# Placing the recurrence's steps by a running count of matrix products beside the gather, and a gate spread over two ticks

## The chip, the cores and the metric

The kernel runs on one core of one Trainium2 chip. The metric is the device time of one execution in microseconds, from the first to the last instruction with what lies around it; lower is better. The core has a matrix engine (PE, with its weight loads listed apart as PEld), a vector engine (DVE), a scalar engine (ACT), a general engine (POOL) and a queue that issues transfers (SP). Each takes its own instructions strictly in the order in which the program wrote them, and waits on semaphores for the others.

## What is computed

Four layers on an input of 8 images x 128 channels x 64 x 64, each on a group-normalised input and added to it:

```python
x = x + layer0(gn(x))   # a state-space scan along 4096 positions, and a 3x3 convolution
x = x + layer1(gn(x))   # four recurrences, below
x = x + layer2(gn(x))   # t3 (two column convolutions) times t4 (a small product)
x = x + layer3(gn(x))   # deformable 3x3 convolution, then a batch norm

# layer 1: down, up, right, left; 63 steps each, every one needs the one before
new = cur + relu(conv1d(prev, w))          # 9 taps along the row

# layer 3: per output pixel 9 taps, each from 4 corners at computed positions
samp = corner(y0, x0, ...) + corner(y0, x0+1, ...) + corner(y0+1, x0, ...) + corner(y0+1, x0+1, ...)
out = einsum(samp * mask, dcn_w)
```

## The kernel before, in words

All is float32. Layer 1 works on four images at once that lie in one tile X, so it runs twice: images 0 to 3, then images 4 to 7. The second run is a generator (`propagate`, called `one`): each `next(one)` writes out one **step**, that is 9 products of 128x128 by up to 256 columns on PE into `ps_l1` (each float32 product is two instructions, 18 in the trace, L913) and one DVE instruction (L920) that adds the result into X. The next step's products read what that DVE instruction wrote. A direction has 63 steps and one turn that only loads weights: 64 turns, 256 in all.

Beside this second run go layer 2 and layer 3 of the first images. The order of the work is written out by hand in **ticks**: one loop over n (before the change its body is at L133 to L155), 96 ticks per image, whatever stands in tick n being written out in this order:

1. `three.tick`, layer 3, from tick 96 on. `fetch` issues 3 gathers (POOL, L1264; an indirect transfer of 128 rows of 2 KB each) into a buffer `got`, of which there are GOT = 6. Then come the parts held back from earlier ticks: `convolve` of four ticks ago (18 PE instructions, L1317, in every sixth tick, n % 6 == 3), `turn` of the fetch two ticks ago (3 PE transposes, L1304, which free the `got` buffer), `keep` (ACT, L1311) and `sum` of the fetch one tick ago (2 DVE additions, L1297). Then `weigh` of this tick's fetch (1 DVE product L1282, 3 ACT products L1286).
2. What `Layer2.plan` puts into the tick for the image that is to be gathered next. Its image has 8 row groups g, four ticks apart (t = 4g): `x2_load` at t-4 (SP), `x2_norm` at t-2 (ACT), `t1_product` at t (PE, L1044), `t4_product` at t+1 (PE, L1058), `t3_start` at t+2 (ACT, L1068), `t3_gate` at t+3 (four DVE instructions, L1073, L1075, L1076, L1077, and the store of the result), `x3_stats` at t+5 (DVE). From tick 36 follow the normalisation, the `tokens` (PE transposes, ACT, table stores), the `offsets` (PE, L1138) and the sampling positions (DVE).
3. A step of layer 1, if the tick has one. In ticks below 96 every third tick has one. From tick 96 to tick `last` = 4 * 96 + 30 = 414 every tick whose number is not a multiple of three has one (`if n % 3: next(one, None)`, L141 to L143 before). At tick 414 any remaining step is written out, and the rest of the loop (ticks to 863) has no steps: X then holds the finished layer 1 and gives way, and later gathers go into pieces of X.

So the part around the change is ticks 96 to 413: image 0 is gathered in ticks 96 to 191 while layer 2 works on image 1, and so on; from tick 384 layer 2 has no work until tick 433. For image 4 (`b == NB2`) two plan times go into one tick. The PSUM buffers that matter: tag `l2a` (two buffers: `ps_t1`, `ps_t3`, `ps_tok`, ...), tag `l2b` (one buffer: `ps_t4`, `ps_off`), `ps_l1` (one), `ps_s` (three). Tile `x2` and tile `t3` have two buffers each.

Of the kernel before, what the change touches and what calls it, by code (L numbers as in the profile page):

```python
# [10 lines left out]
F32 = mybir.dt.float32  # L11
I32 = mybir.dt.int32
AF = mybir.ActivationFunctionType
ALU = mybir.AluOpType
# [3 lines left out]
P = 128  # L18
B, C, H, W = 8, 128, 64, 64
# [5 lines left out]
TR = T // W  # L25
NCH = HW // T
# [13 lines left out]
@with_exitstack  # L40
def conv_preact_kernel(ctx: ExitStack, tc: tile.TileContext, a: dict, out: bass.AP):
    nc = tc.nc
    x_in = a["x"].rearrange("b c h w -> b c (h w)")
    y_out = out.rearrange("b c h w -> b c (h w)")

    const = ctx.enter_context(tc.tile_pool(name="const", bufs=1))
    dram = ctx.enter_context(tc.tile_pool(name="dram", bufs=1, space=DRAM))


    ident = const.tile([P, P], F32, name="ident")  # L50
    make_identity(nc, ident)

    gmat = const.tile([P, P], F32, name="gmat")
    nc.gpsimd.memset(gmat, 0.25)
    gview = gmat.rearrange("p (g q) -> p g q", q=4)
    nc.gpsimd.affine_select(
        out=gview, in_=gview, pattern=[[-4, 32], [0, 4]], compare_op=ALU.is_ge,
        fill=0.0, base=0, channel_multiplier=1,
    )
    nc.gpsimd.affine_select(  # L60
        out=gview, in_=gview, pattern=[[4, 32], [0, 4]], compare_op=ALU.is_ge,
        fill=0.0, base=3, channel_multiplier=-1,
    )
    eps = const.tile([P, 1], F32, name="eps")
    nc.gpsimd.memset(eps, 1e-5)

    x1d = [dram.tile([C, HW], F32, name=f"x1d{b}") for b in range(B)]
    x2d = [dram.tile([C, HW], F32, name=f"x2d{b}") for b in range(B)]
    od = [dram.tile([C, HW], F32, name=f"od{b}") for b in range(B)]
    x3d = [dram.tile([C, HW], F32, name=f"x3d{b}") for b in range(B)]  # L70
    cd = [dram.tile([P, T], F32, name=f"cd{c}") for c in range(B * HW // (4 * T))]
    wide = {
        name: [dram.tile([P, T], F32, name=f"{name}_{i}") for i in range(B * HW // T)] for name in ("dtd", "ud")
    }
    tables = [dram.tile([SIDE * DEEP, 2 * C], F32, name=f"table{b}") for b in range(B)]


    norm1 = const.tile([P, B, 2], F32, name="norm1")
    norm2 = {}
    with tc.tile_pool(name="x", bufs=1) as xp, tc.tile_pool(name="l1w", bufs=1) as wd, tc.tile_pool(  # L80
        name="l1ps", bufs=1, space=PSUM
    ) as pl:
        X = xp.tile([P, HW, NB2], F32, name="X")
        zero = layer0(tc, a, ident, gmat, x_in, x1d, cd, wide, norm1, X, pl)
        one = propagate(tc, a, wd, pl, X)
        edges = borders(tc, X, tables)
        for n in zero:
            with tc.manual_schedule():
                if n >= 0:
                    next(edges, None)  # L90
                if n >= READY:
                    next(one, None)
        with tc.manual_schedule():
            run(edges)
            run(one)

        st = const.tile([P, B * NCH, 6], F32, name="bn_st")
        with tc.tile_pool(name="l2w", bufs=1) as wp, tc.tile_pool(name="l2", bufs=2) as w2, tc.tile_pool(
            name="l3", bufs=2
        ) as w3, tc.tile_pool(name="l2ps", bufs=2, space=PSUM) as p2, tc.tile_pool(  # L100
            name="l3ps", bufs=3, space=PSUM
        ) as p3, tc.manual_schedule():
            st2 = [const.tile([P, NCH, 6], F32, name=f"st2_{b}") for b in range(B)]
            one = propagate(tc, a, wd, pl, X)
            next(one)
            for part in exchange(tc, w3, x1d, x2d, norm1, X, st2):
                if part >= 1:
                    next(one)
                    next(one)
            two = Layer2(tc, a, ident, gmat, eps, x2d, x3d, tables, norm2, wp, w2, p2)  # L110
            three = Layer3(tc, a, ident, tables, od, st, wp, w3, p3)

            def norm_of(b):
                n = group_norm(tc, w2, p2, gmat, eps, st2[b], "l2a")
                keep = const.tile([P, 2], F32, name=f"norm2_{b}")
                for i in range(2):
                    nc.vector.tensor_copy(keep[:, i : i + 1], n[i])
                norm2[b] = keep[:, 0:1], keep[:, 1:2]

            for b in range(NB2):  # L120
                norm_of(b)
            late = residual(tc, w3, x1d, x2d, X, st2, norm_of)

            plans = {}
            for b in range(B):
                for when, what in sorted(two.plan(b).items()):
                    n = b * two.TICKS + when
                    if b == NB2:
                        n = (b + 1) * two.TICKS - (two.TICKS - 5 - when) // 2
                    plans.setdefault(n, []).extend(what)  # L130
            last = NB2 * two.TICKS + 30
            for n in range(min(plans), (B + 1) * two.TICKS):
                b, i = n // two.TICKS - 1, n % two.TICKS  # L133
                if b >= 0:
                    three.tick(b, i, two.done[b], 2 if n < last else 0)
                for f in plans.pop(n, ()):
                    f()
                if n < two.TICKS:
                    if n % 3 == 0:
                        next(one, None)  # L140
                elif n < last:  # L141
                    if n % 3:
                        next(one, None)  # L143
                else:
                    if n == last:
                        run(one)
                        three.bank = pl
                    if n < last + 12 or n % 3 == 0:
                        if next(late, True) and not three.more:
                            size = 3 * 4 * C  # L150
                            flat = X.rearrange("p h b -> p (h b)")
                            for i in range(HW * NB2 // size):
                                piece = flat[:, i * size : (i + 1) * size]
                                three.more.append(piece.rearrange("p (k q c) -> p k q c", k=3, c=C))
                            three.turns = 0  # L155
            run(late)
            while three.late:
                three.tick()
    finish(tc, a, eps, od, x3d, y_out, st, const)
# [663 lines left out]
def run(thread):  # L823
    for _ in thread:
        pass
# [117 lines left out]
class Layer2:  # L943

    TICKS = 96

    def __init__(self, tc, a, ident, gmat, eps, x2d, x3d, tables, norm2, wp, w2, pp):
        self.tc, self.ident, self.gmat, self.eps = tc, ident, gmat, eps  # L950
# [48 lines left out]
    def plan(self, b):  # L999

        nc, w2, pp = self.nc, self.w2, self.pp
        events = {}

        def at(when, f, *args):
            events.setdefault(when, []).append(lambda: f(*args))

        rows = lambda ap: ap.rearrange("p (r w) -> p r w", w=W)
        x2_rows, x3_rows = rows(self.x2d[b]), rows(self.x3d[b])
        S = {}
# [56 lines left out]
        def t3_start(g):  # L1066
            acc = S["acc", g] = pp.tile([P, TR, W], F32, tag="l2a", name="ps_t3")
            nc.scalar.activation(acc, S["t1", g][:, 0:TR, :], AF.Identity, scale=self.w3[:, 0:1])  # L1068

        def t3_gate(g):  # L1070

            acc, t1, t4 = S["acc", g], S["t1", g], S["t4", g]
            nc.vector.scalar_tensor_tensor(acc, t1[:, 1 : 1 + TR, :], self.w3[:, 1:2], acc, ALU.mult, ALU.add)  # L1073
            t3 = w2.tile([P, TR, W], F32, name="t3")
            nc.vector.scalar_tensor_tensor(t3, t1[:, 2 : 2 + TR, :], self.w3[:, 2:3], acc, ALU.mult, ALU.add)  # L1075
            nc.vector.tensor_mul(t4, t3, t4)  # L1076
            nc.vector.tensor_add(t3, S["x2", g][:, 1 : 1 + TR, :], t4)  # L1077
            S["x3", g] = t3.rearrange("p r w -> p (r w)")
            nc.sync.dma_start(self.x3d[b][:, g * T : (g + 1) * T], S["x3", g])
# [124 lines left out]
        for g in range(NCH):  # L1204
            t = 4 * g
            at(t - 4, x2_load, g)
            at(t - 2, x2_norm, g)
            at(t, t1_product, g)
            at(t + 1, t4_product, g)
            at(t + 2, t3_start, g)  # L1210
            at(t + 3, t3_gate, g)
            at(t + 5, x3_stats, g)
        at(36, x3_load, 0)
        at(39, x3_norm_stats)
        for u in range(2):
            t = 44 + 16 * u
# [17 lines left out]
class Layer3:  # L1234
# [59 lines left out]
    def sum(self, got, sums):  # L1294
        for n in range(sums):
            q = 2 - n
            self.nc.vector.tensor_add(got[:, :, 0:q, :], got[:, :, 0:q, :], got[:, :, q : 2 * q, :])  # L1297
# [134 lines left out]
```

## Time and profile before

| | |
|---|---|
| median of 3 runs | 6828.69 us (6819.01 to 6831.93) |
| the profiled execution's own time | 6825.9 us |
| its span, first to last instruction | 6824.2 us |
| mean granted PE clock over the span | 0.877 |
| busy of the span: PE, DVE, ACT, POOL | 81%, 62%, 44%, 64% |
| L913, the steps' products (both runs of layer 1) | 9072 instructions, 2039.9 us |
| L1264, gathers into `got` (into X) | 1614 (690) instructions, 1098 (948) ns each |
| L1282, L1297, DVE per gathered buffer | 1351 ns; 761 ns twice (ticks below 414) |
| L1317, convolutions | 2304 instructions, 590.9 us |

How to read it: the span is that of one execution. "Busy" is the time in which an engine had an instruction in work; idle time stands in front of the instruction that ended it, with what released it. A tick can be found in the trace by counting: there are 768 products L1282, the i-th of them (from 0) is that of tick 96 + i; and the j-th group of three transposes L1304 is written out in tick 98 + j. A tick's length on PE is taken from one such group to the next. In the table by stretches the columns are: from and to, length, then busy time and number of instructions of PE, PEld, DVE, ACT and POOL, then the granted PE clock, the DMA engines' busy share and GB/s.

### The profile page before, as it was taken

To read this page: it belongs to the slowest core of one execution; us is meant where nothing else is said; L and a number is where in the kernel's file an instruction comes from. 1 tells how busy PE (TensorE), PEld (TensorE's weight loads), DVE (VectorE), ACT (ScalarE), POOL (GpSimd) and SP (SyncE) were. 2 spreads that over 40 slices of the span, in tenths; PEclk is the share of its full clock that TensorE was granted. 3 is DMA by queue.
4 is the path that set the end of the run, shared out by engine and by line. 5 is a ranking of instruction groups with operands and counts; after the bars stand their busy time and mean duration, and the time that the engine had idled before them with its cause. 6 is when DMAs were issued, how large, how long until landed. Compare 5 with 4: busy or idle time off the path is not lost. (4 is left out here: it accounts for less than half of the span.)

```text
span 6824.2 us, 76741 instructions
## 1 busy us (share of the span) xinstructions
PE 5519.9 (81%) x25628; PEld 3703.4 (54%) x25628; DVE 4206.7 (62%) x4615; ACT 3000.8 (44%) x5976; POOL 4342.3 (64%) x3758
## 2 busy tenths in 40 slices
PE   4778887799999999899989999977777777876670
PEld 1222222267676767667777777765645555555550
DVE  4889898877777773427677677766542343433235
ACT  4667777655454541313333333333433343433332
POOL 3778787766666662116776776787666666666655
PEclk7777677799999999899999999998888888987775
DMA  4556565544444441525666666667776666676658
GB/s 123 167 173 190 152 182 160 154 133 130 130 130 131 128 132 41 173 80 181 192 191 187 196 191 192 190 178 247 253 223 206 196 212 208 212 213 190 187 164 291
DMA packets 496236, 1195.66 MB, mean 175 GB/s; under 512 B 76248, under 2 KB 117152, under 8 KB 493792
## 3 DMA queue, kind: packets, MB, share of 16 engines
q0 software_dynamic: 184320, 604.13, 30.0%
q1 hardware_dynamic: 300000, 561.43, 26.9%
q10 hardware_dynamic: 11520, 25.18, 1.0%
q8 instruction: 204, 3.34, 0.2%
q14 instruction: 192, 1.57, 0.1%
HBM read 1031.24 MB, written 159.22 MB: 174 GB/s over the span
## 5 line engine op out<-in xcount | busy, mean ns | idle before, releaser
L1264 POOL DMA_INDIRECT got<-table,idx x1614 | 1772.6, 1098 | 1030.1 <-issue 469.4
L913 PE MATMUL ps_l<-X,w_dir 128*128 128x240 f32 (+4 forms) x9072 | 2039.9, 380 | 116.9 <-DVE X L920 75.7
L913 PEld LDWEIGHTS ps_l<-X,w_dir 128*128 128x128 f32 x9072 | 1715.3, 193 | 500.9 <-DVE X L920 186.7
L775 POOL TENSOR_TENSOR hb<-hb,C 128x1024 f32<-128x1024 f32 x512 | 1208.7, 2361 | 41.5 <-POOL carry L774 1.0
L769 DVE TENSOR_TENSOR_SCAN hb<-da,carry,ub_ps 128x512 f32<-128x512 f32 x896 | 1097.8, 1266 | 70.6 <-ACT da L752 13.9
L752 ACT ACTIVATE da<-dt_s,a_neg 128x512 f32<-128x512 f32 x1024 | 678.5, 715 | 569.4 <-DVE hb L769 523.8
L1264 POOL DMA_INDIRECT X<-table,idx x690 | 653.8, 948 | 355.3 <-issue 143.5
L920 DVE SCALAR_TENSOR_TENSOR X<-ps_l,X 128x256 f32<-128x256 f32 x504 | 213.2, 423 | 905.8 <-PE ps_l L913 736.1
L1311 ACT COPY samp<-ps_s 128x384 f32<-128x384 f32 x768 | 365.2, 476 | 860.1 <-remote 455.8
L1304 PE MATMUL ps_s<-ident,got 128*128 128x128 f32 x3594 | 540.9, 295 | 232.1 <-issue 122.7
L1286 ACT ACTIVATE got<-got,wgt 128x128 f32<-128x128 f32 x1614 | 556.7, 400 | 274.7 <-DMA got<-table,idx 220.9
L760 DVE TENSOR_TENSOR ub_ps<-u_s,B_ps 128x1024 f32<-128x1024 f32 x512 | 625.6, 1222 | 82.4 <-PE B_ps L541 52.6
L1317 PE MATMUL ps_o<-samp,dcn_w 128*128 128x256 f32 x2304 | 590.9, 407 | 101.9 <-issue 93.6
L1304 PEld LDWEIGHTS ps_s<-ident,got 128*128 128x128 f32 x3594 | 462.6, 153 | 325.9 <-issue 179.5
L1304 PE MATMUL ps_s<-ident,X 128*128 128x128 f32 x2760 | 424.1, 308 | 187.9 <-issue 166.5
L1317 PEld LDWEIGHTS ps_o<-samp,dcn_w 128*128 128x128 f32 x2304 | 459.7, 204 | 210.5 <-issue 138.5
L774 POOL COPY carry<-hb 128x2 f32<-128x2 f32 x512 | 95.7, 187 | 658.2 <-DVE hb L769 596.4
L1304 PEld LDWEIGHTS ps_s<-ident,X 128*128 128x128 f32 x2760 | 370.9, 161 | 246.8 <-issue 212.3
L1282 DVE TENSOR_TENSOR got<-got,wgt 128x1152 f32<-128x1152 f32 x336 | 453.7, 1351 | 78.0 <-DMA got<-table,idx 70.1
L1297 DVE TENSOR_TENSOR got<-got 128x768 f32<-128x768 f32 x636 | 484.1, 761 | 19.6
L784 PE MATMUL ps_y<-hb,m_y 128*32 128x512 f32 x2048 | 346.2, 742 | 54.4 <-DVE xc L558 41.2
L1282 DVE TENSOR_TENSOR got<-got,wps 128x1152 f32<-128x1152 f32 x202 | 264.4, 1343 | 203.3 <-ACT wps L1278 144.7
(222 smaller groups left out, 6029.8 us busy)
## 6 DMA issues: line engine op xcount, KB each, us to landing
dt_s<-dtd SPq DMA_DIRECT2D x512, 256.0 KB
u_s<-ud SPq DMA_DIRECT2D x512, 256.0 KB
table<-tok SPq DMA_DIRECT2D x128, 256.0 KB
got<-table,idx POOLq DMA_INDIRECT x1614
x<-x2d SPq DMA_DIRECT2D x48, 384.0 KB
x3h<-x3d SPq DMA_DIRECT2D x16, 1056.0 KB
dtd<-dt SPq DMA_DIRECT2D x64, 256.0 KB
ud<-u SPq DMA_DIRECT2D x64, 256.0 KB
```

The source lines that it names most:

```text
L752: nc.scalar.activation(da[:, k], steps[i]["dt"], AF.Exp, scale=a_neg[:, q, k : k + 1])
L760: nc.vector.tensor_mul(ub, st["u"].unsqueeze(1).to_broadcast([P, 2, T]), s["B", h])
L769: nc.vector.tensor_tensor_scan(hb[:, k, :], st["da"][:, k, :], ub[:, k, :], start, ALU.mult, ALU.add)
L775: nc.gpsimd.tensor_mul(hb, hb, S[c]["C", h])
L913: nc.tensor.matmul(ps[:, c0:c1, :], lhsT=w[:, k, :], rhs=v[:, prev, c0 + k - PAD : c1 + k - PAD, :], start=(k == PAD), stop=(k == K - 1),)
L1264: nc.gpsimd.indirect_dma_start(out=got[:, k, :, :].rearrange("p q c -> p (q c)"), out_offset=None, in_=self.tables[b], in_offset=bass.Indi ...
L1282: nc.vector.tensor_mul(got[:, :, 0:3, :], got[:, :, 0:3, :], w.unsqueeze(3).to_broadcast([P, G3, 3, C]))
L1286: nc.scalar.activation(got[:, k, 3, :], got[:, k, 3, :], AF.Identity, scale=wgt[:, t, k0 + k, 3:4])
L1297: self.nc.vector.tensor_add(got[:, :, 0:q, :], got[:, :, 0:q, :], got[:, :, q : 2 * q, :])
L1304: nc.tensor.matmul(ps[:, k, :], lhsT=got[:, k, q, :], rhs=self.ident, is_transpose=True, start=(q == 0), stop=(q == parts - 1),)
L1311: self.nc.scalar.copy(samp[:, k0 : k0 + self.G3, col : col + P], ps)
L1317: nc.tensor.matmul(ps, lhsT=self.dcn_w[:, k, :], rhs=samp[:, k, :], start=(k == 0), stop=(k == KK - 1))
```

## The change

Steps are no longer put into two of three ticks from tick 96 on. A table `load` says for each of the 318 ticks how many units of 128 columns of products it holds without a step: 2 for the transposes, 18 for a convolution, and for layer 2's parts what `PRODUCTS` says. A step is counted as 18. `pace` is the sum of all loads and of all steps still to come, divided by 318. Going through the ticks a running total of loads and placed steps is kept, and steps are written out in a tick as long as the total is half a step behind the pace: none, one or two.

Second, `t3_gate` is cut in two: its first two DVE instructions become `t3_sum` (still at t+3), and the last two and the store stay `t3_gate`, now at t+4; `x3_stats` goes to t+6 and the first `x3_load` to tick 37. No instruction is added or taken away.

```diff
             last = NB2 * two.TICKS + 30
+            STEP = 18
+            first = two.TICKS
+            load = {
+                n: 2 + 18 * (n % 6 == 3) + sum(f.products for f in plans.get(n, ())) for n in range(first, last)
+            }
+            steps, taken, total = 4 * H, 2 * NCH - 1, 0
...
                 if n < two.TICKS:
                     if n % 3 == 0:
-                        next(one, None)
+                        next(one)
+                        taken += 1
                 elif n < last:
-                    if n % 3:
-                        next(one, None)
+                    if n == first:
+                        pace = (sum(load.values()) + STEP * (steps - taken)) / (last - first)
+                    total += load[n]
+                    while total + STEP / 2 <= pace * (n + 1 - first) and taken < steps:
+                        next(one)
+                        taken, total = taken + 1, total + STEP
...
+    PRODUCTS = {"t1_product": 20, "t4_product": 12, "offsets": 14, "tokens": 2, "offsets_out": 2}
...
         def at(when, f, *args):
-            events.setdefault(when, []).append(lambda: f(*args))
+            what = lambda: f(*args)
+            what.products = self.PRODUCTS.get(f.__name__, 0)
+            events.setdefault(when, []).append(what)
...
+        def t3_sum(g):
+            acc, t1 = S["acc", g], S["t1", g]
+            nc.vector.scalar_tensor_tensor(acc, t1[:, 1 : 1 + TR, :], self.w3[:, 1:2], acc, ALU.mult, ALU.add)
+            t3 = S["t3", g] = w2.tile([P, TR, W], F32, name="t3")
+            nc.vector.scalar_tensor_tensor(t3, t1[:, 2 : 2 + TR, :], self.w3[:, 2:3], acc, ALU.mult, ALU.add)
+
         def t3_gate(g):
 
-            acc, t1, t4 = S["acc", g], S["t1", g], S["t4", g]
-            nc.vector.scalar_tensor_tensor(acc, t1[:, 1 : 1 + TR, :], self.w3[:, 1:2], acc, ALU.mult, ALU.add)
-            t3 = w2.tile([P, TR, W], F32, name="t3")
-            nc.vector.scalar_tensor_tensor(t3, t1[:, 2 : 2 + TR, :], self.w3[:, 2:3], acc, ALU.mult, ALU.add)
+            t3, t4 = S["t3", g], S["t4", g]
             nc.vector.tensor_mul(t4, t3, t4)
             nc.vector.tensor_add(t3, S["x2", g][:, 1 : 1 + TR, :], t4)
...
-            at(t + 3, t3_gate, g)
-            at(t + 5, x3_stats, g)
-        at(36, x3_load, 0)
+            at(t + 3, t3_sum, g)
+            at(t + 4, t3_gate, g)
+            at(t + 6, x3_stats, g)
+        at(37, x3_load, 0)
```

## The prediction

> **What bounds the kernel now.** I read the page's slices first, to find the part that the change touches; then the waits in it; then a table of busy times by stretches of ticks; then PE's timeline.
>
> Of the slices (170.6 us each) the 19th to the 27th, 3071 to 4607 us, are ticks 98 to 413: PE at 8 or 9 tenths, DVE and POOL at 7. PE is the fullest engine.
>
> ```profile
> PE   4778887799999999899989999977777777876670
> DVE  4889898877777773427677677766542343433235
> POOL 3778787766666662116776776787666666666655
> ```
>
> By counting L1304's groups of three, tick 98 begins on PE at 3075.90 us and tick 414 at 4608.46. Cut where layer 2 changes its kind of work, the seven stretches are ticks 98 to 129, 130 to 193, 194 to 225, 226 to 289, 290 to 321, 322 to 385 and 386 to 413. First, third and fifth are **dense** (layer 2's products), the others sparse, the last has no layer 2.
>
> ```profile
> 3075.90:3242.05 166.15, 154.21 (x660) 116.17 (x659) 124.09 (x161) 57.72 (x156) 108.93 (x93) 1.00 0.61 187
> 3242.05:3545.03 302.98, 271.00 (x1391) 221.41 (x1390) 205.40 (x262) 115.05 (x308) 223.85 (x191) 0.98 0.64 189
> 3545.03:3713.00 167.97, 157.86 (x678) 119.61 (x676) 124.70 (x162) 58.08 (x157) 114.18 (x98) 1.00 0.65 195
> 3713.00:4012.93 299.93, 270.38 (x1391) 221.59 (x1390) 205.27 (x262) 117.09 (x308) 225.06 (x191) 0.98 0.65 191
> 4012.93:4181.16 168.23, 157.85 (x677) 119.61 (x676) 124.62 (x162) 58.09 (x157) 113.86 (x98) 1.00 0.64 195
> 4181.16:4474.35 293.19, 263.76 (x1368) 217.09 (x1367) 204.18 (x260) 113.28 (x298) 219.33 (x184) 0.98 0.64 187
> 4474.35:4608.46 134.11, 94.72 (x444) 80.78 (x445) 87.13 (x104) 46.74 (x121) 107.91 (x87) 0.91 0.61 179
> ```
>
> The first number after a stretch is its length, the second PE's busy time. The dense ticks take 502.35 / 96 = 5.23 us, PE 94% busy; the sparse ones 896.10 / 192 = 4.67 us, PE 90%; the last 4.79 us, PE 71%.
>
> POOL's groups show that it too is a bound, elsewhere (the first line is ticks 194 to 225, the second ticks 369 to 384):
>
> ```profile
> L1264 POOL DMA_INDIRECT got<-table,idx x98 | 114.8, 1171 | 50.8 <-ACT samp L1311 23.7 <-issue 23.1 <-ACT got L1286 1.2
> ...
> L1264 POOL DMA_INDIRECT got<-table,idx x45 | 55.7, 1237 | 13.7 <-issue 11.0 <-DVE got L1297 1.2 <-DMA got<-table,idx 0.6
> ```
>
> In the dense stretch POOL waits 23.7 us for buffers to be freed (ACT named, but the buffer is freed by PE's transposes). Where 15 ticks have no such wait, only 0.30 us is left before each gather and a tick takes (55.7 + 13.7) / 15 = 4.63 us. So POOL's own pace is 3 x (1.17 to 1.24 + 0.30) = 4.41 to 4.63 us a tick: PE holds the dense ticks, POOL and PE by turns the sparse ones.
>
> PE's timeline in a gather-only stretch shows what PE's idle time is:
>
> ```profile
> 3942.96 4.02 PE L913 MATMUL ps_l<-X,w_dir 128*128 128x256 f32 x18 [0.19 <-DVE X L920]
> 3946.82 0.49 PE L1304 MATMUL ps_s<-ident,got 128*128 128x128 f32 x3
> 3949.00 0.52 PE L1304 MATMUL ps_s<-ident,got 128*128 128x128 f32 x3 [1.69 <-issue]
> 3949.36 3.92 PE L913 MATMUL ps_l<-X,w_dir 128*128 128x256 f32 x18
> ```
>
> A step takes 4.02 us. The tick after it (begun at 3946.82) has no step, and the next transposes come 1.69 us late: the additions that they read stand on DVE behind L920, which waited for the step's end. A step right behind a step costs 0.19.
>
> **The change part by part.** *Steps.* The loads add up to 2718 units, the 208 steps left to 3744; pace 6462 / 318 = 20.32 units a tick. Going through the ticks gives 200 single steps, 4 pairs and 114 ticks without. By stretch: 21, 43, 21, 43, 21, 43, 15 before; 14, 47, 14, 47, 14, 49, 23 after (and tick 97 loses its one). Nothing is added, so PE's busy time moves with the steps.
>
> Dense: PE's busy 469.92 less 21 x 4.02 = 84.4 is 385.5 us, 4.02 us a tick, now below POOL's pace. POOL decides: bounds 4.41 (its mean of this very stretch) and 5.23 (nothing gained). I take 3 x (1.20 + 0.30) = 4.51, between its two rows, since DVE's share goes from 124.70 / 167.97 = 0.74 to about (124.70 - 7 x 0.42) / 144 = 0.84. 96 x 4.51 = 433: **-69 us**.
>
> Sparse: PE's busy 805.14 plus 14 x 4.02 is 861.4. Idle was 91. Each of the three has seven bare ticks with the 1.7 us wait and one of 3.4 (46 in all), which go: nearly all steps now stand in runs of five with the convolution's tick between them, whose 4.05 us cover the wait. Tick 32's 2.84 us x 3 (L920 behind the whole gate) mostly go too, 7. Added: some 0.19s and the pairs, whose second step waits uncovered for L920 (0.42 us) and the way there, 3. Idle 41, sum 902: **+6**. Bounds: no idle, -35; idle as before, +56. Next late here is PE itself, 4.70 us a tick against POOL's 4.41 to 4.63.
>
> Last: PE 94.72 + 8 x 4.02 = 126.9 and little idle; POOL's row of the stretch before it, 4.63 x 28 = 130. Against 134.11 I count **0**, bounds -5 and +6.
>
> *Gate.* The same four instructions. `t4_product` of the next group needs the `l2b` buffer one tick later; before it stand the transposes and 4.46 us of `t1_product`, against DVE's additions, product and half gate, 1.54 + 1.35 + 1.38 = 4.3 us: covered. If not, the difference per group, under 1 us x 24. The `x2` load on SP waits for the gate, so it goes out about 3 us later (one tick of 4.5 less the 1.5 of the first half); behind it on SP stand only stores. It now has some 3 us less before `x2_norm`, 6.3 us in the tightest groups before (issue at 3600.93, norm at 3607.20), and a load of that size took 5.4 us (4735.12 to 4740.5). ACT may wait 2 us per group, with its copies behind it; ACT is 36% busy and `ps_s` has three buffers: 0, at worst 36. For image 4 the gate goes into the next pair of ticks: 0, at worst 8 x 1.4 = 11; there and beyond, the tail's gathers set the pace and nothing is moved.
>
> Sum: -69 + 6 + 0 = -63 us; 6825.9 - 63 = 6763. The median stands 2.8 above the profiled execution: **6766 us**.
>
> [...]
>
> **The rivals.**
> 1. *Given back*: the dense ticks gain, but the sparse stretches take it, as PE there has 14 more steps and its waits stay (idle 91, +56, or half of it with the dense ticks at 4.63, -58). For: tick 50's 10 us of slow `offsets` and DVE's work in ticks 74 to 82 aren't touched. Against: the 1.69s have no cause left. -58 + 28: about 6799.
> 2. *More*: POOL gains a lead in the sparse ticks (it ran up to 23 us ahead of DVE in dense ticks) and spends it in the dense ones; these run at PE's 4.02 plus 0.2, 405 us, -97, sparse -10: about 6722. Against: PE and POOL are within 5% of each other, and such engines hold each other up.
> [...]
> 4. *Not what it says*: the count is wrong, so the placement is uneven. A unit is 4.02 / 18 = 0.223 us; `t1_product` at 20 fits its 4.46 us, but `offsets` are counted 14 and take 66.6 us for 18, that is 3.70 us or 16.6 units. It misplaces about one step per image, a few us, within the forecast.
>
> **How the numbers follow.** Forecast (6740 to 6790) 0.50; more 0.14; given back 0.20, down to no change 0.06; slower 0.10. About 0.2% (14 us) is what a measurement here can tell from no change. Faster 0.84, same 0.06, slower 0.10. Range 6715 to 6822: it takes in *more* and *given back* and leaves out the slower end and part of the same.
>
> **What would show it.** Dense ticks at 4.4 to 4.6 us with POOL's waits for freed buffers (124.5 us over ticks 98 to 413, named ACT samp) under 40; L1264's mean 1.17 to 1.25 there; the 1.69 us waits before L1304 gone and PE's idle in the part down from 162.8 to about 95 us; tick 414 at 4545. Wrong if the mean gather passes 1.44, if sparse ticks pass 4.9 us, or if the time after tick 414 grows.

## The result and the profile after

The changed kernel takes 6762.43 us (median of 4 runs, 6748.84 to 6771.65) against 6826.16 (4 runs, 6819.01 to 6831.93): a ratio of 0.9909 [0.9891, 0.9926], that is 64 us less. The profiled execution took 6766.6 us, its span is 6764.9 us, 59.3 less than before's. In its trace the lines have moved: the steps' products are L924 (were L913), their DVE addition L931 (L920), the gathers L1282 (L1264), the transposes L1322 (L1304), `keep` L1329 (L1311), the ACT products into `got` L1304 (L1286), the convolution L1335 (L1317).

The slices of PE, DVE and POOL, over the changed kernel's whole span:

```profile
PE   4778887899999999799999998997777777866660
DVE  4889898877777774327677676765542333423235
POOL 3778787766666662106777777776666666666655
```

The ticks from 98 on still begin in the 19th slice; POOL and DVE are now at 6 or 7 in nearly all of them, PE at 9. The table by stretches says more. It is cut at the same ticks as before's (98, 130, 194, 226, 290, 322, 386, 414, found by the transposes), with the same columns: length, then busy time of PE, PEld, DVE, ACT, POOL, clock, DMA share, GB/s.

```profile
3069.47:3213.82 144.35, 134.20 (x551) 96.28 (x550) 120.09 (x153) 58.98 (x159) 106.46 (x92) 0.99 0.67 200
3213.82:3516.68 302.86, 283.18 (x1444) 231.53 (x1443) 207.49 (x268) 111.07 (x305) 226.75 (x191) 0.98 0.66 196
3516.68:3663.93 147.25, 137.34 (x569) 100.18 (x568) 120.98 (x154) 59.93 (x161) 109.77 (x96) 0.99 0.68 204
3663.93:3968.61 304.68, 282.08 (x1445) 230.23 (x1444) 207.28 (x268) 115.26 (x305) 229.64 (x194) 0.99 0.67 198
3968.61:4119.88 151.27, 137.79 (x570) 100.44 (x569) 120.79 (x154) 59.85 (x161) 111.46 (x98) 0.98 0.68 202
4119.88:4424.06 304.18, 281.50 (x1459) 233.44 (x1458) 206.79 (x267) 109.27 (x303) 227.03 (x194) 0.99 0.67 196
4424.06:4547.37 123.31, 119.91 (x589) 104.34 (x588) 87.72 (x110) 39.46 (x117) 94.70 (x82) 1.00 0.64 184
```

The first, third and fifth line are the dense stretches: together 442.87 us, were 502.35 (**-59.5**); PE has 60.6 us less work there (409.33 against 469.92). The sparse ones (second, fourth, sixth) are 911.7, were 896.1 (**+15.6**), with 41.6 us more work on PE. The last is 123.3, was 134.1 (**-10.8**): PE's idle time there fell from 39.4 us to 3.4. Tick 98 begins 6.4 us earlier, and what follows tick 414 is 1.8 us longer. -59.5 + 15.6 - 10.8 - 6.4 + 1.8 = -59.3.

POOL's groups, first for ticks 194 to 225 (by PE's transposes), then for 4340 to 4411 us, 48 gathers in a gather-only stretch (busy time, mean ns of one gather, idle time before it and what ended it):

```profile
L1282 POOL DMA_INDIRECT got<-table,idx x96 | 110.3, 1149 | 37.7 <-issue 27.7 <-ACT samp L1329 6.7 <-ACT got L1304 1.5
```

```profile
L1282 POOL DMA_INDIRECT got<-table,idx x48 | 56.9, 1185 | 14.6 <-issue 12.8 <-DMA got<-table,idx 0.6 <-PE ps_s L1322 0.6
```

In the dense stretch the wait for freed buffers is 6.7 us, was 23.7: POOL is hardly held up by PE any more. In the sparse one there is 0.30 us ahead of each gather, as before, and the pace is (56.9 + 14.6) / 16 = 4.47 us a tick (4.63 before, with longer gathers). Over ticks 98 to 413 the waits named ACT samp are 67.2 us, were 124.5.

PE's timeline in a gather-only stretch:

```profile
3899.55 0.49 PE L1322 MATMUL ps_s<-ident,got 128*128 128x128 f32 x3
3900.23 4.02 PE L924 MATMUL ps_l<-X,w_dir 128*128 128x256 f32 x18 [0.19 <-DVE X L931]
3904.09 0.49 PE L1322 MATMUL ps_s<-ident,got 128*128 128x128 f32 x3
3904.77 4.02 PE L924 MATMUL ps_l<-X,w_dir 128*128 128x256 f32 x18 [0.19 <-DVE X L931]
3908.62 4.05 PE L1335 MATMUL ps_o<-samp,dcn_w 128*128 128x256 f32 x18
3912.51 0.49 PE L1322 MATMUL ps_s<-ident,got 128*128 128x128 f32 x3
3912.84 3.92 PE L924 MATMUL ps_l<-X,w_dir 128*128 128x256 f32 x18
```

Steps now stand in runs, the convolution's tick without a step between them, and the 1.69 us before the transposes has gone: such waits (ACT got named) are 5.2 us in the part, were 65.7.

### The profile page after: what moved, and what is told of

Its sections match the earlier page's. It is cut to its first block, busy times and chain, and to the rows that moved or that the text cites. A ratio compares the mean times of both kernels' runs of the same rounds, so it can differ in the third digit from the quotient of the medians.

```text
span 6764.9 us, 76721 instructions
## 1 busy us (share of the span) xinstructions
PE 5512.1 (81%) x25628; PEld 3693.0 (55%) x25628; DVE 4198.0 (62%) x4615; ACT 2985.4 (44%) x5976; POOL 4328.6 (64%) x3758
## 5 line engine op out<-in xcount | busy, mean ns | idle before, releaser
L1282 POOL DMA_INDIRECT got<-table,idx x1614 | 1757.7, 1089 | 983.1 <-issue 460.1
L924 PE MATMUL ps_l<-X,w_dir 128*128 128x240 f32 (+4 forms) x9072 | 2040.6, 380 | 126.6 <-DVE X L931 74.2
L924 PEld LDWEIGHTS ps_l<-X,w_dir 128*128 128x128 f32 x9072 | 1710.2, 192 | 502.1 <-DVE X L931 189.7
L1282 POOL DMA_INDIRECT X<-table,idx x690 | 653.9, 948 | 359.4 <-issue 142.8
L931 DVE SCALAR_TENSOR_TENSOR X<-ps_l,X 128x256 f32<-128x256 f32 x504 | 213.6, 424 | 904.6 <-PE ps_l L924 695.7
L1329 ACT COPY samp<-ps_s 128x384 f32<-128x384 f32 x768 | 365.8, 476 | 926.3 <-PE ps_s L1322 455.7
L1322 PE MATMUL ps_s<-ident,got 128*128 128x128 f32 x3594 | 553.9, 297 | 184.9 <-issue 142.1
L1335 PE MATMUL ps_o<-samp,dcn_w 128*128 128x256 f32 x2304 | 576.2, 402 | 94.5 <-issue 82.9
L1322 PEld LDWEIGHTS ps_s<-ident,got 128*128 128x128 f32 x3594 | 468.5, 154 | 297.5 <-issue 213.0
L1304 ACT ACTIVATE got<-got,wgt 128x128 f32<-128x128 f32 x1614 | 544.4, 400 | 104.5 <-DMA got<-table,idx 78.9
L1335 PEld LDWEIGHTS ps_o<-samp,dcn_w 128*128 128x128 f32 x2304 | 456.0, 202 | 198.7 <-issue 126.3
L1322 PE MATMUL ps_s<-ident,X 128*128 128x128 f32 x2760 | 409.9, 304 | 169.8 <-issue 156.1
L1322 PEld LDWEIGHTS ps_s<-ident,X 128*128 128x128 f32 x2760 | 364.4, 159 | 219.1 <-issue 190.5
L1300 DVE TENSOR_TENSOR got<-got,wgt 128x1152 f32<-128x1152 f32 x336 | 453.1, 1350 | 4.8 <-DMA got<-table,idx 4.5
L1351 DVE BATCH_NORM_STATS2 bn_st<-o_out 128x6 f32<-128x512 f32 x64 | 43.9, 686 | 568.1 <-ACT o_out L1345 463.6
```

Of the source, the lines that this page charges most:

```text
L924: nc.tensor.matmul(ps[:, c0:c1, :], lhsT=w[:, k, :], rhs=v[:, prev, c0 + k - PAD : c1 + k - PAD, :], start=(k == PAD), stop=(k == K - 1),)
L1282: nc.gpsimd.indirect_dma_start(out=got[:, k, :, :].rearrange("p q c -> p (q c)"), out_offset=None, in_=self.tables[b], in_offset=bass.Indi ...
L1300: nc.vector.tensor_mul(got[:, :, 0:3, :], got[:, :, 0:3, :], w.unsqueeze(3).to_broadcast([P, G3, 3, C]))
L1304: nc.scalar.activation(got[:, k, 3, :], got[:, k, 3, :], AF.Identity, scale=wgt[:, t, k0 + k, 3:4])
L1322: nc.tensor.matmul(ps[:, k, :], lhsT=got[:, k, q, :], rhs=self.ident, is_transpose=True, start=(q == 0), stop=(q == parts - 1),)
L1329: self.nc.scalar.copy(samp[:, k0 : k0 + self.G3, col : col + P], ps)
```

## The experiments

Theory A: the dense ticks were bound by PE at 5.23 us, POOL's own pace is 4.4 to 4.6, and the gain is the PE work moved from the first to the stretches with room, so that counting layer 2's products is what matters. Theory B: the gain is the 1.69 us waits of bare ticks (a tick behind a step that has no step and hardly any products itself, with no convolution ahead of the next transposes), which the new placement covers. Theory C: the gate over two ticks frees DVE, and that is part of it.

The runs were made on several chips, on some of which the part after tick 414 is some 300 us shorter for every kernel; so ratios to the kernel before on the same chip are compared, and stretch lengths only beside them.

### One half of the change at a time

`pace_only` has the new placement and the old gate. `gate_only` has the old placement and the new gate:

```diff
+        def t3_sum(g):
...
         def t3_gate(g):
...
-            at(t + 3, t3_gate, g)
-            at(t + 5, x3_stats, g)
-        at(36, x3_load, 0)
+            at(t + 3, t3_sum, g)
+            at(t + 4, t3_gate, g)
+            at(t + 6, x3_stats, g)
+        at(37, x3_load, 0)
```

> The steps placed by the running count, the gate in one tick as before. If the gain is the placement's (my theory), nearly all of it stays: only tick 32, where a step stood behind the whole gate (2.84 us of PE idle in each of three images), and a few dense ticks with a step right behind the gate come back, some 7 us: about 6769, dense ticks 4.65 us. If the gate on two ticks carries it (rival), the time is that of before, 6826, or near it.

> The gate over two ticks, the steps in two of three ticks as before. My theory: the 2.84 us at tick 32 go, three times, and nothing else: about 6819, PE idle in ticks 98 to 413 some 155 us of 163. The rival (the gate carries the gain): under 6790.

Measured: `pace_only` 0.9896 [0.9879, 0.9913], `gate_only` 1.0024 [1.0014, 1.0034]. The placement alone gives the whole gain; the gate alone costs 0.24%, some 15 us. `pace_only` came lower than expected (6769 us would be 0.992), with dense ticks of 4.45 us instead of 4.65; for `gate_only` a small gain had been expected. Theory C falls as an account of the gain. Where most of the 15 us are is seen in PE's waits of `gate_only` (us in total, times, longest):

```profile
PE ps_l L913 <- DMA w_dir<-in_w_up: 5.1, 1, 5.1
PE ps_l L913 <- DMA w_dir<-in_w_left: 5.0, 1, 5.0
PE ps_l L913 <- DMA w_dir<-in_w_right: 4.9, 1, 4.9
```

Before, the same three waits were 1.6, 1.7 and 1.4 us. They are the weights of the next direction. SP's timeline at one of them, and then PE's:

```profile
3637.59 0.32 SPq L1082 DMA_DIRECT2D x3d<-t  x1
3638.01 0.37 SPq L1016 DMA_DIRECT2D x<-x2d  x1
3638.43 0.45 SPq L903 DMA_DIRECT2D w_dir<-in_w_right  x1
```

```profile
3640.35 0.49 PE L1308 MATMUL ps_s<-ident,got 128*128 128x128 f32 x3
3645.78 6.88 PE L913 MATMUL ps_l<-X,w_dir 128*128 128x256 f32 x18 [4.94 <-DMA w_dir<-in_w_right]
```

Before, the same load and the step behind it:

```profile
3666.34 0.43 SPq L903 DMA_DIRECT2D w_dir<-in_w_right  x1
```

```profile
3673.15 3.99 PE L913 MATMUL ps_l<-X,w_dir 128*128 128x256 f32 x18 [1.44 <-DMA w_dir<-in_w_right]
```

The gate's store goes first, as it does before, but it now goes one tick later; the load behind it leaves SP 1.9 us ahead of PE's transposes (3640.35) where before it left 4.9 us ahead (3666.34, transposes at 3671.22). PE waits 4.94 us for the weights, and the step after the wait takes 6.88 instead of 3.99.

### The waits of the bare ticks

`cover_waits` leaves gate and total number of steps of the kernel before and only shifts a step within each six ticks, so that of the two ticks without a step one has the convolution and the other stands just before it. Bare ticks fall from 38 to 1, while dense ticks keep 20 steps a stretch (were 21):

```diff
-                    if n % 3:
+                    if n % 6 not in (2, 3):
```

`conv_uncounted` is the changed kernel with the convolutions left out of the count, so that steps ignore them; dense stretches keep few steps (14 or 15), but 25 ticks are bare:

```diff
-                n: 2 + 18 * (n % 6 == 3) + sum(f.products for f in plans.get(n, ())) for n in range(first, last)
+                n: 2 + sum(f.products for f in plans.get(n, ())) for n in range(first, last)
```

> Before, but the steps stand in the four ticks of six that are not the convolution's (n % 6 == 3) and not the one ahead of it (2): still two thirds of the ticks everywhere, 20 or 21 per dense stretch and 44 per sparse one, but no tick without a step that is not covered by a convolution, so the 1.69 us waits should go. Theory A (the dense ticks' relief is what counts): dense ticks stay near 5.1 us, the sparse ones fall from 4.67 to 4.5 at best because POOL's 4.41 to 4.63 then holds them: -10 dense, -30 sparse, about 6786. Theory B (the uncovered waits are what counts, where the steps are taken from doesn't matter): the whole gain, about 6762.

> The changed kernel, but the 18 units of a convolution are left out of the count: 15, 46, 15, 46, 14, 48, 24 steps by stretch, nearly as in the changed kernel, but 40 steps stand in convolution ticks and 25 ticks without a step have no cover (changed kernel: 1). Theory A: dense ticks as in the changed kernel (4.6 us), sparse ones 25 x 1.7 = 42 us of PE idle worse where PE is the bound: 6780 to 6804. Theory B: all of the waits are back, so little of the gain is left: 6810 or more. If neither matters and only the move between stretches does: 6762.

Measured: `cover_waits` 0.9989 [0.9979, 0.9999], about 7 us: far from theory B's gain, and less than the 40 us that theory A had given it. `conv_uncounted` 0.9918 [0.9905, 0.9931], some four fifths of the gain of `pace_only` on the same chip (A had expected 22 to 46 us of the 64 to stay). Its profile has the waits back (first line; the second is `pace_only`):

```profile
PE ps_s L1322 <- ACT got L1304: 34.9, 20, 2.3
PE ps_s L1318 <- ACT got L1300: 5.8, 4, 1.9
```

34.9 us against 5.8 in `pace_only`, and yet the kernel is only some 0.2% slower than `pace_only`, whose interval overlaps its own. Theory B falls, and so does the price that the prediction put on the waits. But they are not free. These four kernels were profiled on one chip, `gate_only` being the one with the old placement (us, one execution each):

| | ticks 98 to 413 | dense | sparse | PE idle |
|---|---|---|---|---|
| gate_only | 1507 | 517 | 859 | 146 |
| cover_waits | 1474 | 492 | 854 | 116 |
| pace_only | 1430 | 428 | 880 | 70 |
| conv_uncounted | 1447 | 422 | 893 | 90 |

With the waits back, `conv_uncounted` takes 17 us more than `pace_only`, all of it in the sparse and the last ticks. With them covered, `cover_waits` takes 33 us less than `gate_only`; some 15 us of these are what `gate_only` costs by itself, and 4 are a step that `cover_waits` has in tick 96, ahead of the part. So the profiles give the 38 waits at most some 14 us, the medians 7, and the prediction had counted 46 in the sparse stretches alone. A likely reason, not tested by itself, is that in the sparse ticks POOL's pace (4.41 to 4.63 us) lies just behind PE's.

### How much of layer 2 to count

In `layer2_uncounted` the products of layer 2's row groups count nothing, in `layer2_overcounted` half as much again. All else is the changed kernel. `before_again` and `after_again` are the two kernels themselves, on the same chip.

```diff
-    PRODUCTS = {"t1_product": 20, "t4_product": 12, "offsets": 14, "tokens": 2, "offsets_out": 2}
+    PRODUCTS = {"t1_product": 0, "t4_product": 0, "offsets": 14, "tokens": 2, "offsets_out": 2}
```

```diff
-    PRODUCTS = {"t1_product": 20, "t4_product": 12, "offsets": 14, "tokens": 2, "offsets_out": 2}
+    PRODUCTS = {"t1_product": 30, "t4_product": 18, "offsets": 14, "tokens": 2, "offsets_out": 2}
```

> The kernel before, unchanged, on the chip of these runs, for its profile there: ratio 1.000. By theory A its dense ticks are the longest (5.1 us or more), its sparse ticks 4.4 to 4.7.

> The changed kernel, unchanged, beside the others: ratio 0.991 as at first. If the gate on two ticks costs here what it cost alone (the weights' load late on SP, 0.24%), it is slower than the run with the placement alone (0.9896); if that cost is gone, because the directions now change in sparse ticks, equal to it or up to 0.1% faster.

> The changed kernel with t1_product and t4_product counted as nothing: 22, 40, 22, 40, 22, 40, 20 steps by stretch, so the dense ticks keep the steps they had before. Theory A: dense ticks at 5.1 us and more, most of the gain gone, ratio 0.996 to 1.000. Rival (evenness inside a stretch, and pairs and runs of steps, carry the gain): 0.991 to 0.993.

> The changed kernel with t1_product counted 30 and t4_product 18: 10, 50, 10, 50, 10, 53, 25 steps. Theory A with POOL's pace as the floor: the dense ticks stay at 4.4 to 4.6 us though PE has 4 steps fewer there (16 us per stretch), the sparse ones pay 3 steps each, 12 us per image: ratio 0.995 to 0.997. Rival (PE still holds the dense ticks, more relief gives more): 0.989 or less.

| | steps in the seven stretches | dense, us | sparse, us | last, us | ratio |
|---|---|---|---|---|---|
| before_again | 21, 43, 21, 43, 21, 43, 15 | 508.3 | 907.9 | 115.3 | 0.9993 [0.9978, 1.0008] |
| layer2_uncounted | 22, 40, 22, 40, 22, 40, 20 | 523.8 | 878.5 | 132.5 | 1.0013 [0.9999, 1.0027] |
| after_again | 14, 47, 14, 47, 14, 49, 23 | 439.0 | 916.5 | 125.4 | 0.9913 [0.9896, 0.9929] |
| layer2_overcounted | 10, 50, 10, 50, 10, 53, 25 | 422.8 | 947.2 | 132.2 | 0.9943 [0.9924, 0.9961] |

With layer 2's products not counted the gain is gone, though the steps are still placed by a count and bare ticks are down to 18 (`conv_uncounted` has 25 and keeps the gain): what makes the kernel faster is the count of layer 2. Overcounting (0.995 to 0.997 had been expected) shows the other side. Its dense and sparse stretches 194 to 225 and 226 to 289, and POOL's group in the first:

```profile
3519.30:3662.41 143.11, 122.88 (x498) 86.43 (x496) 117.31 (x149) 60.96 (x160) 111.94 (x98) 0.99 0.72 213
3662.41:3968.93 306.52, 290.07 (x1496) 240.97 (x1497) 210.61 (x272) 111.50 (x305) 226.54 (x192) 0.98 0.67 194
```

```profile
L1282 POOL DMA_INDIRECT got<-table,idx x98 | 113.3, 1156 | 31.5 <-issue 24.1 <-ACT got L1304 2.4 <-ACT o_out L1345 1.9
```

PE is busy for only 86% of the dense stretch, and a tick there still takes 4.47 us: POOL, with 0.32 us ahead of each gather and hardly a wait for freed buffers (0.6 us named ACT samp), is the floor. Four steps fewer per dense stretch than `after_again` gained 16 us in all three, and the sparse stretches, where PE is 93% busy, gave 31 back. Of the three counts the true one is the fastest: against `layer2_overcounted` the medians lie 24 us apart, though the two intervals just overlap. Counts in between were not run.

### The weight load on another queue

To see whether the load behind the gate's store is what makes `gate_only` slower, the second run's weights were loaded from ACT's queue, in each of four kernels: `before_act`, `gate_act`, `pace_act`, `after_act`.

```diff
-            one = propagate(tc, a, wd, pl, X)
+            one = propagate(tc, a, wd, pl, X, nc.scalar)
...
-        nc.sync.dma_start(w, a[name])
+        (queue or nc.sync).dma_start(w, a[name])
```

> The kernel before, but the second run's weights of the next direction are loaded from ACT's queue instead of SP's, so that no store of layer 2 stands ahead of them. The wait for them was 1.4 to 1.7 us, three times: ratio 0.999 to 1.000.

> The gate over two ticks, steps in two of three ticks, weights from ACT's queue. If what made the split gate cost 0.24% is SP's order (the weights' load behind the gate's later store, 5.0 us of waiting instead of 1.5, three times, and a step at half clock after it), the cost is gone and tick 32's 1 to 2 us are left as a gain: ratio 0.998 to 1.000, equal to or below the run before it in this list. Rival (the cost lies on DVE or on the l2b buffer): it stays at 1.002.

> Placement alone with the weights from ACT's queue: the directions change in sparse ticks, where nothing stood ahead of the load on SP, so as without: ratio 0.989 to 0.990.

> Both parts with the weights from ACT's queue. If the split gate is worth nothing beside the placement, equal to the run with the placement alone within 0.1%; if it is worth my 7 us at tick 32 and in the dense ticks, 0.1% faster; if t4_product's waits for the gate's second half (8.2 us in the profile of the changed kernel) are a loss of their own, 0.1% slower.

The load came no earlier from there, so the test is not a clean one. ACT's timeline in `before_act` shows why:

```profile
3162.05 0.59 ACT L1051 COPY t<-ps_t 128x512 f32<-128x512 f32 x1 [7.28 <-PE ps_t L1044]
3162.19 0.34 ACTq L903 DMA_DIRECT2D w_dir<-in_w_up  x1
```

On ACT the load stands behind a copy that waits 7.28 us for `t1_product` on PE; it leaves 2.5 us ahead of PE's transposes (3164.70), all three times, where from SP it left 4.9 us ahead. But the waits were of four sizes, and the time goes with them (for the first row the waits are from the profile of before on another chip):

| | waits for the weights, us | ratio |
|---|---|---|
| before | 1.7, 1.6, 1.4 | 1 |
| before_act | 3.9, 3.9, 2.7 | 1.0012 [1.0002, 1.0021] |
| gate_act | 4.9, 4.6, 3.5 | 1.0016 [1.0007, 1.0024] |
| gate_only | 5.1, 5.0, 4.9 | 1.0024 [1.0014, 1.0034] |

Counted with the step behind each, which is slower too (5.4 to 6.9 us instead of 3.99), the three waits cost 10.8, 13.0 and 18.2 us more than in before's profile, in the order of the rows; the ratios say 8, 10 and 15 us. Against `before_act` the gate cost nothing that can be measured in `gate_act`, with waits nearly alike. That the late load is the cause is thus supported, not proved: a kernel without the wait would need a second weight buffer and was not tried.

`pace_act` is 0.9887 [0.9869, 0.9906], `after_act` 0.9866 [0.9848, 0.9885], the lowest ratio of all. Its three dense stretches are alike; the third:

```profile
3927.46:4064.16 136.70, 135.07 (x569) 99.08 (x568) 120.74 (x154) 60.23 (x161) 108.33 (x94) 1.00 0.73 216
```

4.27 us a tick with PE idle for 1.6 us in all. Against `pace_act` (140.7, 141.9 and 143.8) the split gate looks worth some 4 to 7 us per dense stretch here; but the sparse stretches took 10 us more (890.6 against 880.6), and the intervals of the two ratios overlap; so beside the new placement the split gate is worth between nothing and some 0.4%, and whether the ACT queue adds to that stays open, as `after_act` and the changed kernel did not run on one chip.

## Why the prediction was right, point by point

The forecast was 6766 us; 6762.43 came. The sum was right within 4 us, and the mechanism is shown by the runs: the dense ticks were PE's (`layer2_uncounted` leaves them PE's and loses the gain), and behind PE stands POOL (`layer2_overcounted`). The terms were less good than their sum: the dense and the sparse ticks came 9.5 and 9.6 us dearer than forecast, the last stretch and the start 10.8 and 6.4 us cheaper, and that these nearly cancel is luck.

- **Dense, -69 forecast, -59.5 measured.** The tick was forecast as 3 x (1.20 + 0.30) = 4.51 us; it was 4.61, against gathers of 1.14 to 1.16 us, shorter than assumed. That gathers lengthen with DVE's share, the reason given for 1.20, the runs do not show as a rule: the mean was 1.17 us at a share of 0.74 to 0.75 before, 1.14 to 1.16 at 0.80 to 0.83 here, 1.18 to 1.22 at 0.84 in `pace_only` and 1.15 to 1.16 at 0.88 in `after_act`. So POOL's pace was 3 x (1.15 + 0.30) = 4.35, and 0.26 us a tick, 25 us in all, is waits that the forecast did not have: POOL's for freed buffers are still 7.8, 6.7 and 6.0 us in the three stretches, some of them behind stalls as the one shown at the end. In `after_again` the same ticks took 69.3 us less than in `before_again`, in `after_act` a tick took 4.27: the waits differ from run to run. PE's 4.02 us a tick was too low as well; it was 409.33 / 96 = 4.26. Of the 21 turns of a dense stretch before, one only loads weights and has no products, and after the change these turns fall into sparse stretches. So the products of 18 steps left the dense ticks, not of 21, and their busy time there fell by 67.0 us (237.2 to 170.2), not by 84.4. PE thus stood close to POOL's pace in the dense ticks too.
- **Sparse, +6 forecast, +15.6 measured.** Two steps failed, in opposite directions. PE's busy time rose by 41.6 us and not by 14 x 4.02 = 56.3, since for the reason just given only 11 steps with products came in (129 to 140). And "Idle 41" was 65 us. The waits named ACT got did go, from 36.0 us in these stretches to 5.3; but steps waiting for L931 rose from 18.2 us to 27.7 (the forecast had "3"), so that of the 31 us taken out 9.5 came back at once, and idle fell by 26, not by 50. Nor is the price of a wait its length: covering the bare waits with hardly any work moved gave 7 us (`cover_waits`).
- **Last, 0 forecast, -10.8 measured.** The step that failed is PE's 126.9. It takes before's 94.72 us as so much work; but before's were measured at a mean granted clock of 0.91, with 39.4 us of PE idle time in the stretch, after's at 1.00, with 3.4. At after's mean, 119.91 us for 589 instructions, before's 444 come to 90.4 and eight steps of 18 to 29.3, together 119.7. POOL's row gave 130, and the stretch took 123.3, 4.40 us a tick. How much of this is the change is not sure: `before_again` took 115.3 where before took 134.1, and on its chip the changed kernel took 125.4.
- **Start, not counted, -6.4.** Tick 97 lost its step, as the working said in passing without a price. Tick 98 begins between 3053.95 and 3075.90 in the four profiles of the two kernels, so its size can't be told.
- **Gate, 0 forecast.** "behind it on SP stand only stores" was wrong: the next direction's weights stand there too. Alone this cost 0.24%; in the changed kernel directions end in other ticks, and the waits named are 1.7 and 1.3 us. Whether it still costs something there is not told: `after_again` at 0.9913 and `pace_only` at 0.9896 overlap, on two chips. "covered" for `t4_product` held mostly: PE waited for the gate's second half five times, 8.2 us in all.
- **Rivals.** *Given back* is `layer2_overcounted` in kind, not this kernel. *More* (PE at 4.02 + 0.2 a tick) came in `after_act`, 4.27 a tick, and in its dense ticks alone. *Slower*, given 0.10, was that the dense stretches' gathers lengthen with VectorE's share of the time; it needed a mean of 5.23 / 3 - 0.30 = 1.44 us. The share rose to 0.83, 0.82 and 0.80 (120.09 / 144.35 and so on) and to 0.88 in `after_act`, but mean gathers fell to 1.157, 1.149 and 1.143 us (1.171 before) and were 1.22 at most in `pace_only`, never near the 1.44. Gathers beside DVE's product of a fetch were the longer ones: in before's dense stretches the 123 that overlapped no L1282 took 0.94 to 0.95 us each, the 164 that did took 1.34 on average; in the changed kernel's (the product is L1300 there) 103 took 0.94 to 0.95 and 181 took 1.26 on average. So more gathers met the product, but took less time beside it on average; why is not shown. *Not what it says* (`offsets` counted as 14 units for some 16.6) was not tested.
- **What would show it**: dense ticks of 4.4 to 4.6 us came as 4.61; POOL's waits "under 40" were 67.2, of which 20.5 stand in the dense stretches; PE's idle "about 95" was 101.9; tick 414 at 4545 was at 4547.37.

## What to carry to other kernels

Where the order is written by hand, add up each engine's work over stretches of the length that its buffers can bridge, and move free work away from stretches where one engine is fullest until the next engine's pace is reached; past that point it is given back where the work goes (16 us gained and 31 given back in `layer2_overcounted`). Idle gaps of an engine say little on their own: 38 gaps of 1.7 us were worth 7 us here by the medians and at most some 14 by the profiles, probably because another engine stood right behind. And when a store is moved on an in-order queue, list all that is issued behind it, also what belongs to another layer (in `gate_only` PE's waits for the next direction's weights went from some 1.5 to 5.0 us).

## What the runs showed of the hardware

- A short wait on PE can cost more than its length. In `gate_only` PE waited 4.94 us for weights, and the 18 instructions behind took 6.88 us instead of 4.02. The table of those two stretches gives the granted clock in the third column from the right, 0.92 and then 0.56:

```profile
3640.00:3645.78 5.78, 0.84 (x5) 0.36 (x4) 3.74 (x5) 2.89 (x8) 4.42 (x5) 0.92 0.90 293
3645.78:3652.50 6.72, 6.72 (x18) 5.61 (x19) 0.00 (x0) 0.60 (x3) 1.76 (x2) 0.56 0.54 188
```

  In before's run, with a wait of 1.44 us at this place, the clock was 1.00 and the step took 3.99. The wait's length alone does not decide: in before's trace a step behind a wait of 2.77 us (at 4477.63) took 5.71 us at a mean clock of 0.70, and one behind 2.76 us (at 4562.09) took 4.02 at 1.00; in the changed kernel one behind 3.53 us (at 4304.79) took 4.02 at 1.00.
- PE, ACT and DVE can stop together for a few microseconds while POOL goes on, with no cause in the trace. In the changed kernel DVE's timeline has, in the fourth stretch:

```profile
3923.98 1.35 DVE L1300 TENSOR_TENSOR got<-got,wgt 128x1152 f32<-128x1152 f32 x1
3931.56 0.42 DVE L931 SCALAR_TENSOR_TENSOR X<-ps_l,X 128x256 f32<-128x256 f32 x1 [6.22 <-remote]
```

  The step that L931 waits for had begun at 3922.07 and takes 4.02 us, so some 5.5 us are left over; ACT is idle for 5.89 us at the same time, and POOL went on to issue gathers until 3929.9. The ends of PE's instructions are modelled in the trace, so the step may have run longer than it shows. PE's own waits are 5.62 us here and 6.63 us nine steps later; in `after_again` the same two steps waited 5.64 and 6.49 us, in `after_act` neither did, and other such stalls stand in one run only. They are a good part of the idle time that the forecast lacked. Their cause stays open.
- Weights loaded from ACT's queue, where they stood behind a copy that waited 7.28 us, were waited for 2.7 to 3.9 us (`before_act`); from SP's queue, 1.4 to 2.0 us (before and `before_again`). The kernels differ in nothing else, but the profiles are of different chips.
